# A four-layer graph network on one core: table look-ups as float32r parts, and a row-by-row dilation in blocks of 32 rows on GpSimd

## The chip, the core and the metric

The kernel runs on one core of a Trainium2 chip. A core has five engines with an instruction queue each: TensorE (PE, matrix products; PEld is its weight load), VectorE (DVE), ScalarE (ACT), GpSimd (POOL) and SyncE (SP, which here only issues DMA transfers). Each engine works its queue off in order and waits on semaphores for the others. The metric is the time of one execution on the device in microseconds (us), the median of several runs.

## The reference, cut to what matters

There are 16 graphs of 1024 nodes with 128 features and a 0/1 adjacency `adj` of 1024x1024 per graph. Four layers follow one another, each of the form `x = layernorm(x + layer(x, adj))`:

- layer 0: attention with relu projections, masked by `adj`;
- layer 1: a maximum over neighbours. With `q = x W2`, each node takes `max_j adj[i,j] * relu(p_i + q_j + b)`;
- layer 2: a sum over neighbours and two dense layers;
- layer 3: three rounds of neighbour averaging, normalisation and batch norm, on a *dilated* adjacency.

The dilation depends on `adj` alone, and it is sequential. For each row n, in order:

```
row  = carry[n]                 # earlier rows' removals are already in it
num  = sum(row)
sf   = (num + 1) // 2 if num > 10 else 1
rm   = row & (cumsum(row) % sf == 0)     # none if num <= 1 or masked
carry[n]    = row & ~rm
carry[:, n] = carry[:, n] & ~rm          # also in the later rows
```

So row n removes its neighbours of rank sf and 2 sf (or all of them), and what it removes in column n changes the counts and ranks of the later rows.

## The kernel before

**Layers 0 to 2** (function `layers_012`) run graph by graph. The loop over the graphs calls `max_conv(b)` for layer 1. Its inner loop has 147 groups `g` of 7 nodes each. For every 21 groups DVE builds `sub`, the maxima of all 128 subsets of 7 values of `q` (line 270). Three groups at a time are transposed by PE (line 277) and copied by ACT to an SBUF tile `table` (line 279, three buffers). For each group, PE counts with a bf16 product which subset of the 7 nodes each of the 1024 nodes has as neighbours (`pm`, line 284, a PSUM tile with one buffer), ACT turns that into the 0/1 tile `hot` (line 286), PE looks the maxima up by a product of `table` and `hot` in float32 (`pg`, line 150, called from `look_up`), and DVE takes the running maximum `best` (line 262).

After every group, `between(g)` puts in pieces of other work: layer 2 of the graph before (`gin`), layer 0 of the graph after (`attention`), and the dilation, a generator that yields after each piece. `pieces` and `slots` spread its pieces evenly over the 16 x 147 groups in the order of the source. The framework then schedules each engine's queue itself, by data dependences and its own estimates, so the order on an engine can differ from that of the source.

**The dilation** works in 8 blocks of 128 rows of all graphs. A block loads its rows as bytes (`E`, partition = row in the block, graph and column in the free dimension) and the squares on the diagonal (`Dg`, partition = graph). It takes off what earlier blocks removed (`rp`, transposed by PE, line 353, subtracted by DVE, line 354), counts the rows outside the square by ACT (lines 356 and 360), and then does 127 steps, one per row, on 16 partitions, all on DVE (lines 374 to 387): a running count over the 128 columns of the square (a scan), five instructions on one element per graph, three over the row, and one over the column below, in bytes. The square goes back to `E` through DRAM (`own`, lines 391 and 392), ACT counts again (line 396), and a scan over the whole row with an ACT instruction and one DVE instruction (lines 413 to 416) marks what each row removes. That is stored to `removed` (line 418).

GpSimd has little to do: `off` for attention (line 219), the small vectors of `layernorm` and its 8 wide instructions (lines 161 to 171), and the loads that convert a type.

**Layer 3** reads `removed` per graph in one transfer (`gone_all`, line 492), takes it and its transpose off the adjacency (`dilated`, lines 499 and 500), and runs `sage` per graph and round, with two reciprocals on DVE in the first round (`deg`, line 513, and `inv`, line 532). `deg` is stored as `share` (line 514).

Of the kernel before, what the change touches and what calls it, by code (L numbers as in the profile page):

```python
# [26 lines left out]
F32 = mybir.dt.float32  # L28
BF = mybir.dt.bfloat16
# [7 lines left out]
P = 128  # L37
# [5 lines left out]
TG = 21  # L43
LOWEST = -(2.0**100)
# [17 lines left out]
def tile_graph_layers(ctx: ExitStack, tc, a, out):  # L62
# [11 lines left out]

    def bank(name, dtype=F32):
        return psum.tile([P, 2048 // (2 if dtype == BF else 4)], dtype, tag="bank", name=name, bufs=2)

# [44 lines left out]
    mask_u = consts.tile([B, N], U8, name="mask_u")  # L122
    nc.sync.dma_start(out=mask_u, in_=a["nodemask"])
    half_mask = consts.tile([B, N], F32, name="half_mask")
    nc.vector.tensor_scalar(half_mask, mask_u, 0.5, None, op0=ALU.mult)
    nm = consts.tile([P, T, B], F32, name="nm")
    half_nm = consts.tile([P, T, B], F32, name="half_nm")
# [3 lines left out]
    nc.vector.tensor_copy(half_nm.rearrange("p t b -> p (t b)"), pm[:, :T * B])  # L131
    nc.vector.tensor_scalar_mul(nm, half_nm, 2.0)
# [3 lines left out]
    removed = [dram.tile([N, N], BF, name=f"removed{b}") for b in range(B)]  # L136
# [16 lines left out]
    def layernorm(dst, src):  # L153
# [9 lines left out]
        gp.tensor_scalar(mean, mean, 0.5, None, op0=ALU.mult)  # L163
# [3 lines left out]
        gp.tensor_scalar(apart, apart, 0.25, None, op0=ALU.mult)  # L167
        gp.tensor_add(var, var, apart)  # L168
        gp.tensor_tensor(rs, var, mhalf, op=ALU.pow)  # L169
        for t in range(T):  # L170
            gp.tensor_scalar(dst[:, t, :], src[:, t, :], mean[:, t:t + 1], rs[:, t:t + 1],  # L171
                             op0=ALU.subtract, op1=ALU.mult)
# [20 lines left out]
    def layers_012():  # L193
# [6 lines left out]
        def attention(b, An):  # L200
# [6 lines left out]
            nc.gpsimd.tensor_scalar_mul(kT, kT, -1.0)  # L207
# [40 lines left out]
        def max_conv(b, AT, between):  # L248
# [8 lines left out]
            def look_up(g, table, hot):  # L257
                pg = product(table, hot, "pg")
                if g == 0:
                    nc.vector.tensor_copy(best, pg)  # L260
                else:
                    nc.vector.tensor_max(best, best, pg)  # L262

            last = None
            for g0 in range(0, NG, TG):
# [6 lines left out]
                for g in range(g0, g0 + TG):  # L272
                    at = (g - g0) % 3
                    if at == 0:
                        pt = bank("pt")
                        for k in range(3):
                            nc.tensor.transpose(pt[:, k * P:(k + 1) * P], sub[:, g - g0 + k, :], ident)  # L277
                        table = w2.tile([P, 3, P], F32, name="table", bufs=3)
                        nc.scalar.copy(table.rearrange("s g o -> s (g o)"), pt[:, :3 * P])  # L279
# [5 lines left out]
                    hot = w2.tile([P, N], F32, name="hot", bufs=2)  # L285
# [3 lines left out]
                    last = g, table[:, at, :], hot  # L289
# [45 lines left out]

        def dilation():
            for k in range(T):
                own = slice(k * P, (k + 1) * P)
                E = dil.tile([P, B, N], U8, name="E")
                nc.gpsimd.dma_start(out=E, in_=adj[:, own, :].rearrange("b p m -> p b m"))  # L340
                Dg = dil.tile([B, P, P], U8, name="Dg")
                nc.gpsimd.dma_start(out=Dg, in_=adj[:, own, own])

                counts = dil.tile([P, 2, B], F32, name="counts")
                nc.vector.memset(counts, 0.0)
                for b in range(B):
                    if k:
                        rp = dil.tile([P, T - 1, P], BF, name="rp", bufs=2)
                        nc.sync.dma_start(out=rp[:, :k, :],
                                          in_=removed[b][:k * P, own].rearrange("(j p) n -> p j n", p=P))  # L350
                        p = bank("pr", BF)
                        for j in range(k):
                            nc.tensor.transpose(p[:, j * P:(j + 1) * P], rp[:, j, :], ident_b)
                        nc.vector.tensor_tensor(E[:, b, :k * P], E[:, b, :k * P], p[:, :k * P], op=ALU.is_gt)
                        junk = dil.tile([P, N], BF, name="junk", tag="gone", bufs=2)
                        nc.scalar.activation(junk[:, :k * P], E[:, b, :k * P], AF.Copy,
                                             accum_out=counts[:, 0, b:b + 1])
                    if k < T - 1:
                        junk = dil.tile([P, N], BF, name="junk", tag="gone", bufs=2)
                        nc.scalar.activation(junk[:, :N - (k + 1) * P], E[:, b, (k + 1) * P:], AF.Copy,  # L360
                                             accum_out=counts[:, 1, b:b + 1])
                    yield
                p = bank("pc")
                for s in range(2):
                    nc.tensor.transpose(p[:B, s * P:(s + 1) * P], counts[:, s, :], ident)
                before = dil.tile([B, P], F32, name="before")
                after = dil.tile([B, P], F32, name="after")
                nc.vector.tensor_scalar_add(before, p[:B, 0:P], 1.0)
                nc.vector.tensor_scalar_add(after, p[:B, P:2 * P], -0.5)
                for n in range(P - 1):  # L370
                    mine = Dg[:, n, :]
                    m = slice(k * P + n, k * P + n + 1)
                    rank1 = small.tile([B, P], F32, name="rank1")
                    nc.vector.tensor_tensor_scan(rank1, mine, mine, before[:, n:n + 1], op0=ALU.add, op1=ALU.max)  # L374
                    sc = small.tile([B, 5], F32, name="sc")
                    half, h1, at, every, at2 = (sc[:, i:i + 1] for i in range(5))
                    nc.vector.tensor_scalar(half, rank1[:, P - 1:P], after[:, n:n + 1], half_mask[:, m],
                                            op0=ALU.add, op1=ALU.mult)
                    nc.vector.tensor_scalar(h1, half, MAGIC, 1.0 - MAGIC, op0=ALU.add, op1=ALU.add)
                    nc.vector.scalar_tensor_tensor(at, half, 5.5, h1, op0=ALU.is_gt, op1=ALU.mult)  # L380
                    nc.vector.scalar_tensor_tensor(every, half, 1.0, at, op0=ALU.is_gt, op1=ALU.is_gt)
                    nc.vector.tensor_scalar(at2, at, 2.0, -1.0, op0=ALU.mult, op1=ALU.add)
                    hit = small.tile([B, P], F32, name="hit")
                    nc.vector.tensor_scalar(hit, rank1, at, every, op0=ALU.is_equal, op1=ALU.max)  # L384
                    nc.vector.scalar_tensor_tensor(hit, rank1, at2, hit, op0=ALU.is_equal, op1=ALU.max)  # L385
                    nc.vector.tensor_mul(hit, hit, mine)
                    nc.vector.tensor_tensor(Dg[:, n + 1:, n], Dg[:, n + 1:, n], hit[:, n + 1:], op=ALU.is_gt)  # L387
                    yield

                Dd = dram.tile([B, P, P], U8, name=f"own{k}")  # L390
                nc.sync.dma_start(out=Dd, in_=Dg)
# [231 lines left out]
```

## Time and profile before

| what | value |
|---|---|
| median of 3 runs | 9725.1 us (9717.61 to 9733.46) |
| the profiled execution's own time | 9721.92 us |
| its span, first to last instruction | 9720.1 us |
| mean granted TensorE clock | 0.932 of full speed |
| PE busy | 8365.7 us, 86% of the span |
| DVE busy | 7624.2 us, 78% |
| ACT busy | 4286.9 us, 44% |
| POOL busy | 1095.8 us, 11%, 1423 instructions |
| stores of `x3` (end of a graph's layer 2), first and last | 679.1 and 7887.9 us |

Busy shares are of the whole span. The first 7888 us belong to layers 0 to 2 with the dilation beside them, the rest to layer 3. Times in the views are microseconds, means are nanoseconds. A group's line gives line, engine, operation, the tiles written and read, shapes, count, busy time and mean, and then the idle time of the engine just before these instructions and what ended most of it. A line of a timeline gives start and length.

### The profile page before, as it was taken

How to read it: one execution, taken by the hardware profiler on the slowest of the kernel's cores; microseconds unless marked ns; L12 is line 12 of the kernel's file. 1: busy time of each engine (PE TensorE's matmuls, PEld its weight loads, DVE VectorE, ACT ScalarE, POOL GpSimd, SP SyncE). 2: the span in 40 equal slices, each digit the busy share in tenths (PEclk: the TensorE clock that was granted, in tenths of full speed). 3: DMA queues.
4: the chain of work that ended last, by engine and by line, in shares of the span. 5: the costliest groups of instructions: out<-in, count | busy, mean ns of one | idle time of the engine just before them, and what ended most of it. 6: DMA issues, size and time to landing. Idle time of an engine off the chain costs nothing. (4 is left out here: it accounts for less than half of the span.)

```text
span 9720.1 us, 86636 instructions
## 1 busy us (share of the span) xinstructions
PE 8365.7 (86%) x29288; PEld 4084.1 (42%) x29288; DVE 7624.2 (78%) x16197; ACT 4286.9 (44%) x5170; POOL 1095.8 (11%) x1423
## 2 busy tenths in 40 slices
PE   7989898999899989898989898989898967778774
PEld 4444444444444444444444444444444433334333
DVE  4998599869886988699859986998699958845454
ACT  3445544554465445444554455445544621122221
POOL 1010101010101010101010101010101010101116
PEclk8999999999999999999999999999999978889886
DMA  3010201020102010201020102010200057733332
GB/s 47 1 22 19 35 1 22 19 37 1 22 20 39 1 22 20 40 1 22 19 43 1 22 18 46 1 22 18 47 1 11 11 159 201 200 115 130 130 130 75
DMA packets 317237, 435.20 MB, mean 45 GB/s; under 512 B 105445, under 2 KB 156792, under 8 KB 316662
## 3 DMA queue, kind: packets, MB, share of 16 engines
q1 hardware_dynamic: 219696, 295.75, 9.2%
q0 software_dynamic: 92560, 132.72, 8.8%
q8 instruction: 230, 3.77, 0.2%
q10 hardware_dynamic: 4534, 1.19, 0.1%
q14 instruction: 217, 1.78, 0.1%
HBM read 461.64 MB, written 119.54 MB: 60 GB/s over the span
## 5 line engine op out<-in xcount | busy, mean ns | idle before, releaser
L150 PE MATMUL pg<-hot,table 128*128 128x512 f32 x9408 | 4548.7, 605 | 134.4 <-DVE best L262 42.8
L286 ACT ACTIVATE hot<-pm,one_less 128x1024 f32<-128x1024 f32 x2352 | 2617.1, 1113 | 2235.1 <-PE pm L284 2080.4
L262 DVE TENSOR_TENSOR best<-best,pg 128x1024 f32<-128x1024 f32 x2336 | 2828.8, 1211 | 534.5 <-PE pg L150 530.4
L150 PEld LDWEIGHTS pg<-hot,table 128*128 128x128 f32 x9408 | 1729.4, 191 | 1770.3 <-issue 1137.5
L284 PE MATMUL pm<-AT,lit 126*128 126x512 bf16 x4704 | 1437.2, 385 | 190.9 <-ACT hot L286 101.3
L284 PEld LDWEIGHTS <-lit 126*128 126x128 bf16 x4704 | 461.0, 99 | 1099.8 <-issue 1067.1
L279 ACT COPY table<-pt 128x384 f32<-128x384 f32 x784 | 373.3, 477 | 816.5 <-PE pt L277 811.5
L219 POOL TENSOR_SCALAR off<-An 128x1024 bf16<-128x1024 bf16 x128 | 164.2, 1283 | 3578.7 <-PE psc L223 3183.0
L277 PE MATMUL pt<-ident,sub 128*128 128x128 f32 x2352 | 410.8, 283 | 178.3 <-DVE sub L270 88.6
L189 PE MATMUL pagg<-m,part 128*128 128x512 bf16 x2304 | 529.0, 382 | 34.9 <-DVE inv L530 25.4
L277 PEld LDWEIGHTS pt<-ident,sub 128*128 128x128 f32 x2352 | 304.4, 146 | 516.6 <-issue 270.2
L374 DVE TENSOR_TENSOR_SCAN rank<-Dg,before 16x128 f32<-16x128 uint8 x1016 | 498.4, 491 | 27.2
L270 DVE TENSOR_TENSOR sub<-sub,q 128x21 f32<-128x21 f32 (+6 forms) x784 | 434.9, 555 | 49.3 <-ACT q L252 43.9
L387 DVE TENSOR_TENSOR Dg<-Dg,hit 16x127 uint8<-16x127 uint8 (+63 forms) x1016 | 454.2, 447 | 24.5
L189 PEld LDWEIGHTS <-part 128*128 128x128 bf16 x3072 | 298.2, 98 | 394.9 <-issue 53.4
L385 DVE SCALAR_TENSOR_TENSOR hit<-rank,sc,hit 16x128 f32<-16x128 f32 x1016 | 348.1, 343 | 25.6
L557 PE MATMUL pl<-w_L_gnn_Wl,hT 128*128 128x128 f32 x768 | 199.1, 367 | 178.6 <-ACT hT L581 113.2
L178 ACT CAST part<-left 128x1024 bf16<-128x1024 f32 x128 | 133.7, 1044 | 482.9 <-DVE left L180 482.8
L384 DVE TENSOR_SCALAR hit<-rank,sc 16x128 f32<-16x128 f32 x1016 | 342.7, 337 | 0.0
L532 DVE RECIPROCAL inv<-inv 128x1024 f32<-128x1024 f32 x48 | 314.3, 6548 | 19.3 <-ACT inv L531 19.3
L560 DVE SCALAR_TENSOR_TENSOR x<-pl,nm,x 128x128 f32<-128x128 f32 x384 | 129.5, 337 | 252.2 <-PE pl L557 161.4
L171 POOL TENSOR_SCALAR X<-y,ln_mv 128x128 f32<-128x128 f32 x384 | 319.4, 848 | 5.2
(172 smaller groups left out, 8512.2 us busy)
## 6 DMA issues: line engine op xcount, KB each, us to landing
m<-kept SPq DMA_DIRECT2D x32, 2048.0 KB, 9.4
An<-in_adj_dram POOLq DMA_DIRECT2D x16, 2048.0 KB, 14.3
removed<-gone SPq DMA_DIRECT2D x128, 256.0 KB, 2.0
m<-in_adjT_dram POOLq DMA_DIRECT2D x16, 2048.0 KB, 13.6
gone_all<-removed SPq DMA_DIRECT2D x16, 2048.0 KB, 9.7
kept<-m SPq DMA_DIRECT2D x16, 2048.0 KB, 14.2
AT<-in_adjT_dram POOLq DMA_DIRECT2D x16, 2016.0 KB, 14.6
hidden<-r SPq DMA_DIRECT2D x48, 512.0 KB, 3.8
```

The costliest lines, as they stand in the source:

```text
L150: nc.tensor.matmul(p[:, s], lhsT, rhs[:, s], start=True, stop=True)
L189: nc.tensor.matmul(p[:, s], parts[k][:, c, :], m[:, c, s], start=(c == 0 and k == 0), stop=(c == T - 1 and k == 2))
L262: nc.vector.tensor_max(best, best, pg)
L270: nc.vector.tensor_max(sub[:, :, n:2 * n], sub[:, :, 0:n], qg[:, g0:g0 + TG, k:k + 1].to_broadcast([P, TG, n]))
L277: nc.tensor.transpose(pt[:, k * P:(k + 1) * P], sub[:, g - g0 + k, :], ident)
L279: nc.scalar.copy(table.rearrange("s g o -> s (g o)"), pt[:, :3 * P])
L284: nc.tensor.matmul(pm[:, s], lit[:rows, r, :], AT[:rows, c, s], start=True, stop=True)
L286: nc.scalar.activation(hot, pm, AF.Relu, bias=one_less)
L374: nc.vector.tensor_tensor_scan(rank1, mine, mine, before[:, n:n + 1], op0=ALU.add, op1=ALU.max)
L384: nc.vector.tensor_scalar(hit, rank1, at, every, op0=ALU.is_equal, op1=ALU.max)
L385: nc.vector.scalar_tensor_tensor(hit, rank1, at2, hit, op0=ALU.is_equal, op1=ALU.max)
L387: nc.vector.tensor_tensor(Dg[:, n + 1:, n], Dg[:, n + 1:, n], hit[:, n + 1:], op=ALU.is_gt)
```

## The change

**Look-up.** The transposed table goes to two tiles of type float32r, a shortened float32 for PE. ACT copies it to `high` (which rounds) and, whole, to `whole`; GpSimd writes the difference to `low`. `hot` becomes float32r too. `look_up` makes four float32r products per group (two halves, `high` and `low` each) in place of two in float32.

**Dilation.** Blocks have 32 rows instead of 128, so there are 32 blocks. Four graphs are packed on 128 partitions: partition = 32 g + row, with graph = 4 q + g. Loads come one block ahead, and the next block is prepared by the generator `prepare` among the steps of the current one. DVE ranks the ones above the diagonal of the 32x32 squares once per block and writes to `V` (through DRAM, partition = graph) for each such pair its rank from the row's start in the square, or a large number where there is no pair. A step then no longer needs the row itself, only the count `low` of what lies before the diagonal and the count `rest` of the whole row: ten GpSimd instructions, six on one element per graph and four on the rest of the row. The hits of a block go back through DRAM, DVE transposes them in 32x32 squares, and the whole-row part at the end of a block is as before, but with four rows of 1024 per block and partition and with DVE transposing the removals (`last_T`, stored to `removed_T`) in place of PE. `pieces` follows the new count.

**Elsewhere.** `layernorm` and the negation of `kT` use multiply and add on GpSimd. Sixteen small transfers fill `half_rows` at the start. `gone_all` comes in four transfers of 32 partitions each, since `removed` is laid out by block.

The core of the diff:

```diff
-            def look_up(g, table, hot):
-                pg = product(table, hot, "pg")
+            def look_up(g, parts, hot):
+                pg = wide("pg")
+                for s in halves:
+                    for k, part in enumerate(parts):
+                        nc.tensor.matmul(pg[:, s], part, hot[:, s], start=(k == 0), stop=(k == 1))
...
-                        table = w2.tile([P, 3, P], F32, name="table", bufs=3)
-                        nc.scalar.copy(table.rearrange("s g o -> s (g o)"), pt[:, :3 * P])
+                        high = w2.tile([P, 3 * P], F32R, name="high", bufs=2)
+                        nc.scalar.copy(high, pt[:, :3 * P])
+                        whole = w2.tile([P, 3 * P], F32, name="whole")
+                        nc.scalar.copy(whole, pt[:, :3 * P])
+                        low = w2.tile([P, 3 * P], F32R, name="low", bufs=2)
+                        nc.gpsimd.tensor_sub(low, whole, high.bitcast(F32))
...
-                    hot = w2.tile([P, N], F32, name="hot", bufs=2)
+                    hot = w2.tile([P, N], F32R, name="hot", bufs=2)
...
-                for n in range(P - 1):
-                    mine = Dg[:, n, :]
...
-                    nc.vector.tensor_tensor_scan(rank1, mine, mine, before[:, n:n + 1], op0=ALU.add, op1=ALU.max)
...
-                    nc.vector.tensor_mul(hit, hit, mine)
-                    nc.vector.tensor_tensor(Dg[:, n + 1:, n], Dg[:, n + 1:, n], hit[:, n + 1:], op=ALU.is_gt)
+                gp = nc.gpsimd
+                for n in range(R - 1):
+                    if n % 4 == 3 and k + 1 < K:
+                        next(ahead, None)
+                    m = slice(k * R + n, k * R + n + 1)
+                    mine = low[:, n:n + 1]
+                    sc = small.tile([B, 6], F32, name="sc")
+                    half, sf, none, at, to = (sc[:, i:i + 1] for i in range(5))
+                    gp.tensor_scalar(half, mine, half_mask[:, m], rest[:, n:n + 1], op0=ALU.mult, op1=ALU.add)
+                    gp.tensor_scalar(sf, half, MAGIC, -MAGIC, op0=ALU.add, op1=ALU.add)
+                    gp.tensor_scalar(sf, half, 5.5, sf, op0=ALU.is_gt, op1=ALU.mult)
+                    gp.tensor_scalar(none, half, 1.0, FAR, op0=ALU.is_le, op1=ALU.mult)
+                    gp.tensor_sub(at, mine, sf)
+                    gp.tensor_scalar(to, at, sf, none, op0=ALU.subtract, op1=ALU.subtract)
+                    last = small.tile([B, R], F32, name="last_rank")
+                    gp.tensor_scalar(hit[:, n, n + 1:], V[:, n, n + 1:], at, None, op0=ALU.is_equal)
+                    gp.tensor_scalar(last[:, n + 1:], V[:, n, n + 1:], to, None, op0=ALU.is_le)
+                    gp.tensor_add(hit[:, n, n + 1:], hit[:, n, n + 1:], last[:, n + 1:])
+                    gp.tensor_sub(low[:, n + 1:], low[:, n + 1:], hit[:, n, n + 1:])
                     yield
...
-            gp.tensor_scalar(dst[:, t, :], src[:, t, :], mean[:, t:t + 1], rs[:, t:t + 1],
-                             op0=ALU.subtract, op1=ALU.mult)
+            gp.tensor_scalar(dst[:, t, :], src[:, t, :], rs[:, t:t + 1], mean[:, t:t + 1],
+                             op0=ALU.mult, op1=ALU.add)
...
-        pieces, slots, done = T * (3 * B + P - 1), B * NG, 0
+        pieces, slots, done = K * (R + 8), B * NG, 0
...
-        nc.sync.dma_start(out=gone, in_=removed[b].rearrange("(c p) i -> p c i", p=P))
+        q, g = divmod(b, G)
+        rows = removed[:, g * R:(g + 1) * R, q, :].rearrange("(c k) r i -> k r c i", c=T)
+        for k in range(P // R):
+            nc.sync.dma_start(out=gone[k * R:(k + 1) * R], in_=rows[k])
```

## The prediction, made before the changed kernel ran

> **What bounds the kernel now.** I read the page's busy shares, then stretches of time, the costliest groups, one stretch of the timeline, and last GpSimd's (POOL's) own timeline. Layers 0 to 2 run from 0 to 7888 us (the last store of `x3` is issued there, line 331); layer 3 takes the other 1832 us. One graph of layers 0 to 2 has 147 look-up groups, which I call slots. From the first `x3` store (679.1) to the fifteenth (7505.6) there are 14 graphs: 487.6 us each. The busy time by stretches of 240 us, columns length, PE, PEld, DVE, ACT, POOL, clock, DMA:
>
> ```profile
> 1200.00:1440.00 240.00, 221.64 (x764) 107.20 (x762) 230.01 (x599) 111.56 (x130) 10.69 (x8) 0.99 0.00 1
> 1440.00:1680.00 240.00, 212.85 (x675) 97.43 (x675) 218.19 (x614) 102.98 (x112) 35.35 (x55) 0.95 0.11 23
> 1680.00:1920.00 240.00, 222.74 (x751) 109.51 (x750) 210.69 (x448) 138.00 (x170) 15.02 (x9) 0.97 0.08 14
> 1920.00:2160.00 240.00, 211.50 (x728) 102.98 (x729) 146.04 (x198) 127.96 (x186) 34.74 (x56) 0.94 0.25 43
> ```
>
> Of two graphs, three stretches have DVE at 210 to 230 of 240 us and PE at 213 to 223: two engines near their limit. The fourth, without dilation steps, has PE alone at 212. POOL is nearly empty. The groups that matter (times, busy and mean, idle before):
>
> ```profile
> L150 PE MATMUL pg<-hot,table 128*128 128x512 f32 x9408 | 4548.7, 605 | 134.4 <-DVE best L262 42.8
> L286 ACT ACTIVATE hot<-pm,one_less 128x1024 f32<-128x1024 f32 x2352 | 2617.1, 1113 | 2235.1 <-PE pm L284 2080.4
> L262 DVE TENSOR_TENSOR best<-best,pg 128x1024 f32<-128x1024 f32 x2336 | 2828.8, 1211 | 534.5 <-PE pg L150 530.4
> ...
> L279 ACT COPY table<-pt 128x384 f32<-128x384 f32 x784 | 373.3, 477 | 816.5 <-PE pt L277 811.5
> ...
> L374 DVE TENSOR_TENSOR_SCAN rank<-Dg,before 16x128 f32<-16x128 uint8 x1016 | 498.4, 491 | 27.2
> ```
>
> One slot in a stretch without dilation:
>
> ```profile
> 2004.16 0.60 PE L284 MATMUL pm<-AT,lit 126*128 126x512 bf16 x2
> ...
> 2004.59 1.88 PE L150 MATMUL pg<-hot,table 128*128 128x512 f32 x4
> 2004.85 1.11 ACT L286 ACTIVATE hot<-pm,one_less 128x1024 f32<-128x1024 f32 x1 [1.04 <-PE pm L284]
> ...
> 2006.31 0.60 PE L284 MATMUL pm<-AT,lit 126*128 126x512 bf16 x2
> ```
>
> Start to start, two bf16 products take 0.43 us (0.215 each) and the two f32 products, four records, 1.72 us (0.43 a record). The period is 2.15; with the transposes (0.32 start to start per three slots, 0.11 a slot) 2.26. PE sets it and ACT waits. `hot` starts 0.69 after `pm` and runs 1.11, and `pm` has one buffer.
>
> POOL's small instructions, in a quiet stretch (start, length):
>
> ```profile
> 117.18 0.24 POOL L163 TENSOR_SCALAR ln_mv<-ln_mv 128x8 f32<-128x8 f32 x1
> 117.38 0.20 POOL L164 TENSOR_TENSOR ln_mv<-ln_mv 128x8 f32<-128x8 f32 x1
> 117.66 0.20 POOL L166 TENSOR_SCALAR ln_mv<-ln_mv 128x8 f32<-128x8 f32 x1
> 117.95 0.24 POOL L167 TENSOR_SCALAR ln_mv<-ln_mv 128x8 f32<-128x8 f32 x1
> 118.27 0.20 POOL L168 TENSOR_TENSOR ln_mv<-ln_mv 128x8 f32<-128x8 f32 x1
> 118.55 1.68 POOL L169 TENSOR_TENSOR ln_mv<-ln_mv,mhalf 128x8 f32<-128x8 f32 x1
> ```
>
> From 164 on, where each needs a result just made, starts lie 0.28, 0.29, 0.32 and 0.28 apart. The step of the new dilation is such a chain.
>
> **Part 1: DVE is relieved.** The ten step instructions (lines 374 to 387) were busy 2778 us, 174 per graph. DVE was busy 6299.6 of the 7480 us from 120 to 7600, 411 per graph; 237 stay. The new block work adds little: per block some 25 instructions of at most 128 elements, nearest the 16x1 to 16x128 rows (134 to 343 ns), about 6 us, and four transposes of up to 992 bf16 elements, by the 672-element row (0.86 us) at most 1.3 us each; the other forms shrink or stay. Even at 260 us DVE no longer sets the end.
>
> **Part 2: the look-up.** Four f32 records of 0.43 become four float32r matmuls. The trace has no such operand. Its bounds are the bf16 product (0.215) and the f32 record (0.43). I take 0.215: an f32 product costs four bf16 ones, as when both operands are cut in two, and here the kernel does the cutting itself, with one matmul per part. A slot then asks PE for 0.43 + 0.86 + 0.11 = 1.40 us. What is late next is the loop of the one `pm` buffer: 0.69 + 1.11 + about 0.06 for the release = 1.86 us. ACT has 0.69 free in it, into which one table copy (0.48) fits; there are now two per three slots, so I add 0.48 / 3 = 0.16: 2.02 us a slot.
>
> By the Trainium skill, page FP8 and Floating Point Precision, section TensorE Precision Notes, true FP32 takes four passes and FP32 can be read at reduced precision instead. The four passes agree with 0.86 against 0.215 us here; the page names no float32r, and no run yet shows the reduced read. One pass is the sum as I make it, two are the second rival below.
>
> **Part 3: a step on POOL.** Ten instructions, nine of which need the result before them. At the spacing above: 9 x 0.29 + 0.17 (the distance of independent ones) = 2.8 us. Four of them are on 31 down to 1 elements, 16 on average: the row of `inv` (line 535, 128x1024, 2828 ns) against 0.20 for 8 elements gives 2.6 ns an element, so 4 x 16 x 2.6 = 0.17. That is 2.95 us. Seven operands are per-partition scalars read from SBUF. Line 171 has two of them on 128 elements and a median of 803 ns: 128 x 2.6 = 333 and 0.22 leave 0.25, so 0 to 0.13 each. Step: 2.95 to 3.85 us; I take 3.3, since line 171 also has a second operation that may take that rest.
>
> The Trainium skill, GPSIMD Engine Reference, section 4.1 Engine selection, speaks against the move: elementwise work belongs on VectorE, with GpSimd about twice as slow for two inputs. Here DVE's 16x1 instructions took 134 to 158 ns and POOL's 200 to 240, 1.5 times. Twice 145 ns would be 2.9 us a step as an estimate, about 400 us less in the whole than my 3.3.
>
> **Part 4: where the steps stand.** This decides. Every third slot `low<-whole,high` is now queued on POOL, and PE can't look up without it. Its cost: 0.20 + 376 x 2.6 ns = 1.17 us. In POOL's order of the built program a graph in the middle has 49 of these and two blocks of 31 steps, but the steps are not spread: the 31 stand in runs of 19, 7, 1, 4 in one block and 1, 13, 6, 5, 6 in the other, with one `low` between runs. Only 7 of the 49 lie inside blocks, 42 (126 slots) outside. `low` and `high` have two buffers, `whole` one. So while POOL works off 19 steps (63 us), PE has two tables at most, 12 us of work, and then waits. The cover that hid `low` is gone there; the queue behind a step is every `low`, `off` and load on POOL, and behind those PE, ACT and DVE. Block time and slot time add:
>
> - blocks: 62 x 3.3 = 204.6, and 7 x 1.17 = 8.2: 213 us;
> - 126 slots x 2.02 = 254.5;
> - other ACT work, in the same loop: ACT was busy 3694 of 7480 us, 241 a graph, of which `hot` and table were 187; 54 are left, less the old counts (lines 356, 360 and 396: some 354 us, 22 a graph), plus the new ones (128 of about 0.8 us, 6.5): 38.5;
> - seams between graphs: PE was busy 6765.8 of 7480 us, so it waited 46.5 us a graph, which I keep.
>
> Sum 552.8 against 487.6: 65.2 x 16 = **+1043 us**.
>
> **Part 5: the ends.** Layer 3's first pass took 37.7 us a graph (`deg` on DVE, line 513, at 8133.38 and 8171.05). Each graph's `gone_all` comes in four loads now, and in SP's order the fourth stands behind the `share` store of the graph before, thus behind the reciprocal `deg` (line 513, 6.54 us). That exposes up to the landing (9.7 us, line 492) plus the 6.5: 0 to 16 us a graph. I take 12: +192. The layernorm's 8 wide instructions change to multiply-add, whose row (`off`, 1283 ns for 1024) gives about 0.4 instead of 0.80 us; where POOL sets the end (9561 to 9715 us) that is up to 16 x 8 x 0.4 = 51, I take -42. Sixteen more loads on POOL ahead of the first `An` cost about 1 us each by line 427's row (1017 ns): +15. The wait of hits for their two hops through DRAM (own's hops: 3.8 and 3.9 us) lies under the 21 tables between blocks, some 130 us: nothing; without that cover it is 32 x 8 = 256.
>
> Sum: 9720.1 + 1043 + 192 - 42 + 15 = 10,928 us. The profiled run's own time was 9721.92 and the median 9725.1, so +5: **10,930 us**.
>
> **Rivals.**
> 1. *Faster: a POOL step is cheap.* Only 16 of 128 partitions and mostly one element; independent instructions start 0.17 apart. The point: 62 s + 348 = 487.6 - 10 (part 5) gives s = 2.1 us. At 1.6 us, ten at 0.16: 10,930 - 62 x 1.7 x 16 = 9,240. Against: one element still took 228 ns (line 546), and dependent starts in that stretch never lay under 0.28. Chance 0.08.
> 2. *float32r at 0.43.* PE sets the slot again: 0.43 + 1.72 + 0.11 = 2.26, so 126 x 0.24 = 30 a graph, +484: 11,415. For: every f32 record, the transposes too (0.107 per 128 columns), runs at half the bf16 rate. Chance 0.15.
> 3. *Scalar operands at 0.13 each.* s = 3.85: +546, 11,475. For: line 171. Chance 0.17.
>
> **How the numbers follow.** The forecast has 0.60, from 2.4 to 3.5 us a step. The low end is 2.4 us, where the wait on the result before cost almost nothing: -893, 10,040, rounded to 10,000. The high end, 11,750, holds each of rivals 2 and 3 and a part of both together (11,960). Outside are rival 1 and the rest of that. What a measurement of this kernel can tell from no change is about 0.2%, 20 us. Faster 0.07, same 0.01 (rival 1 near its point), slower 0.92.
>
> **What would show it.** POOL busy near half the span with some 10,000 instructions of 0.2 to 0.35 us; PE's wait for `low` on POOL at the head of the waits, in pieces of 10 to 50 us, 100 us or more a graph; DVE near half busy; a graph's period near 550 us with two stretches of about 100 us in which PE is nearly idle and its clock may fall; the look-up's records 0.215 apart, and `hot` still waiting for `pm`. I am wrong if POOL's step is under 2.1 us, or if PE's waits for POOL are short.

## The result and the profile after

| | before | changed |
|---|---|---|
| median of the comparison's runs | 9721.35 us (9717.45 to 9733.46) | 11144.93 us (11134.22 to 11147.04) |
| ratio to before, 95% interval | | 1.146 (1.144 to 1.148) |
| span of the profiled execution | 9720.1 us | 11132.5 us |
| mean granted TensorE clock | 0.932 | 0.808 |
| layers 0 to 2, last store of `x3` | 7887.9 us | 9080.2 us |
| a graph, first to fifteenth store, 14 graphs | 487.6 us | (8703.15 - 802.7) / 14 = 564.3 us |
| layer 3, from that last store to the end | 1832 us | 2052 us |

The change is slower by 14.6%. The prediction was 10,930 us, 2% below what was measured. The page after, busy shares and four rows of slices:

```profile
PE 7135.3 (64%) x28909; PEld 4339.3 (39%) x29144; DVE 5552.6 (50%) x7044; ACT 4337.4 (39%) x5498; POOL 4462.2 (40%) x12357
...
PE   5666666666666666666666666666666655558776
...
DVE  3545454545454545454544545454545455555555
...
POOL 5444544444444444444444444444444510001114
```

DVE fell from 78% to 50%, as the edit says it should, and yet the kernel is longer. No engine is near full in any slice of layers 0 to 2. That is the look of a kernel that waits. The groups that answer to those of before (busy and mean, then idle before and its releaser):

```profile
L290 DVE TENSOR_TENSOR best<-best,pg 128x1024 f32<-128x1024 f32 x2336 | 2843.8, 1217 | 3221.7 <-PE pg L286 3195.7
...
L286 PE MATMUL pg<-hot,low 128*128 128x512 f32 x4704 | 2031.4, 435 | 2100.1 <-POOL low L311 2100.1
...
L311 POOL TENSOR_TENSOR low<-whole,high 128x384 fp32r<-128x384 f32 x784 | 799.4, 1020 | 2510.9 <-ACT whole L309 2401.9
```

`low` itself takes 1.02 us, 50 us a graph. But PE stood 2100.1 us idle before the products with `low`, and the view of waits gives the longest piece:

```profile
PE pg L286 <- POOL low L311: 2100.1, 230, 49.2
...
ACT whole L309 <- POOL low L311: 1403.1, 146, 44.5
```

Columns are the sum, the number and the longest. These are 131 us a graph, and few waits make it: of 15 in the graph that ends at 7001 us, five last 11 to 49 us and 119 us together. What POOL does meanwhile is a step, and the next, with no `low` between them. One step in POOL's timeline (start, length), from line 469 to the next line 469:

```profile
3001.82 0.32 POOL L469 TENSOR_SCALAR sc<-low_counts,half_mask,rest 16x1 f32<-16x1 f32 x1
...
3003.43 0.37 POOL L474 TENSOR_SCALAR sc<-sc 16x1 f32<-16x1 f32 x1
...
3004.77 0.19 POOL L479 TENSOR_TENSOR low_counts<-low_counts,hit 16x9 f32<-16x9 f32 x1
3005.07 0.33 POOL L469 TENSOR_SCALAR sc<-low_counts,half_mask,rest 16x1 f32<-16x1 f32 x1
```

It lasts 3.25 us here, 3.5 us on the longest rows, 3.33 on average where nothing comes between; I use 3.35. And PE in the same block, at the end of such a wait:

```profile
2983.59 0.58 PE L286 MATMUL pg<-hot,high 128*128 128x512 f32 x1
2995.33 0.80 PE L286 MATMUL pg<-hot,low 128*128 128x512 f32 x1 [11.17 <-POOL low L311]
2995.93 0.63 PE L286 MATMUL pg<-hot,high 128*128 128x512 f32 x1
2996.35 0.63 PE L286 MATMUL pg<-hot,low 128*128 128x512 f32 x1
...
3001.65 0.40 PE L286 MATMUL pg<-hot,low 128*128 128x512 f32 x1
3001.88 0.39 PE L286 MATMUL pg<-hot,high 128*128 128x512 f32 x1
```

PE gets one `low`, works off three slots in 8 us, and waits for the next `low` behind the next run of steps (11.5 us at 3015.12). The second thing to see is the spacing: 0.42 us right after the wait, 0.23 us six microseconds later. I come back to that in the last section.

### The profile page after: what moved, and what is told of

Same layout as the page of the kernel before. It is cut to its first block, busy times and chain, and to the rows that moved or that the text cites. A ratio compares the mean times of both kernels' runs of the same rounds, so it can differ in the third digit from the quotient of the medians.

```text
span 11132.5 us, 90950 instructions
## 1 busy us (share of the span) xinstructions
PE 7135.3 (64%) x28909; PEld 4339.3 (39%) x29144; DVE 5552.6 (50%) x7044; ACT 4337.4 (39%) x5498; POOL 4462.2 (40%) x12357
## 5 line engine op out<-in xcount | busy, mean ns | idle before, releaser
L318 ACT ACTIVATE hot<-pm,one_less 128x1024 fp32r<-128x1024 f32 x2352 | 2621.2, 1114 | 2793.6 <-PE pm L316 1726.8
L286 PE MATMUL pg<-hot,low 128*128 128x512 f32 x4704 | 2031.4, 435 | 2100.1 <-POOL low L311 2100.1
L286 PE MATMUL pg<-hot,high 128*128 128x512 f32 x4704 | 2402.0, 514 | 133.7 <-DVE e L252 67.6
L286 PEld LDWEIGHTS pg<-hot,low 128*128 128x128 f32 x4704 | 990.5, 211 | 2363.4 <-POOL low L311 2184.4
L311 POOL TENSOR_TENSOR low<-whole,high 128x384 fp32r<-128x384 f32 x784 | 799.4, 1020 | 2510.9 <-ACT whole L309 2401.9
L286 PEld LDWEIGHTS pg<-hot,high 128*128 128x128 f32 x4704 | 971.8, 208 | 610.1 <-DVE best L290 100.8
L309 ACT COPY whole<-pt 128x384 f32<-128x384 f32 x784 | 382.8, 488 | 1404.5 <-POOL low L311 1403.1
L307 ACT CAST high<-pt 128x384 fp32r<-128x384 f32 x784 | 373.0, 476 | 329.5 <-PE pt L305 297.4
L474 POOL TENSOR_SCALAR sc<-sc 16x1 f32<-16x1 f32 x992 | 374.7, 378 | 109.6
L476 POOL TENSOR_SCALAR hit<-V,sc 16x31 bf16<-16x31 bf16 (+30 forms) x992 | 347.7, 351 | 0.0
L471 POOL TENSOR_SCALAR sc<-sc 16x1 f32<-16x1 f32 x992 | 289.1, 291 | 108.2
```

Of the source, the lines that this page charges most:

```text
L286: nc.tensor.matmul(pg[:, s], part, hot[:, s], start=(k == 0), stop=(k == 1))
L307: nc.scalar.copy(high, pt[:, :3 * P])
L309: nc.scalar.copy(whole, pt[:, :3 * P])
L311: nc.gpsimd.tensor_sub(low, whole, high.bitcast(F32))
L318: nc.scalar.activation(hot, pm, AF.Relu, bias=one_less)
L474: gp.tensor_scalar(to, at, sf, none, op0=ALU.subtract, op1=ALU.subtract)
```

## The experiments

My theory after the result had a narrow and a wide form. Narrow: only `low`, queued behind steps, costs the time. Wide: GpSimd works its queue in order, so whatever is computed on GpSimd or issued from it stands behind a run of steps, and every engine stands behind that. The rivals were that the block-wise dilation is slow wherever its steps run, that GpSimd's work slows VectorE, and that layer 3 is slow for a reason of its own. Periods below are always from the first to the fifteenth `x3` store, over 14 graphs; some of the expectations have 492, 425 and 540 us for kernels that have 490.0, 432.0 and 552.3 by this measure. A time without a range is that of one execution; kernels that ran four to seven times spread by 0.1 to 0.3%.

**The look-up alone.** The kernel before with the float32r tables (`rank1` and `hit` have one buffer, for space).

```diff
-                        table = w2.tile([P, 3, P], F32, name="table", bufs=3)
...
+                        high = w2.tile([P, 3 * P], F32R, name="high", bufs=2)
...
+                        nc.gpsimd.tensor_sub(low, whole, high.bitcast(F32))
```

> The old dilation (blocks of 128 rows, steps on DVE) with the new look-up: high and whole copied by ACT, low on GpSimd, four float32r products a group. To make room, rank1 and hit of the old steps have one buffer each. Theory (GpSimd's queue is the cause): GpSimd carries no steps, so low comes on time; PE's group costs 1.40 us in place of 2.26, but DVE stays near its limit (411 of 487.6 us a graph), so the period falls only a little, to 455 to 485 us, and the time is 9250 to 9700 us; PE's waits for low are under 100 us in all. Rival (the look-up itself costs, through two copies and a third engine): period above 500, time above 9900 us.

Measured 9862.6 us (before in this comparison: 9726.45), 1.4% slower. The period was 497.2 us, the last store came at 7866.1 as before, and what remained of the dilation delayed layer 3: its first `deg` stood at 8073.0 instead of 7931.1. I had expected a gain, and that was a miss. DVE stayed at 79% with the old steps, so a shorter slot on PE had little to give: with these steps on DVE the look-up was not what set the end. And the steps themselves grew, from 2778 to 3034 us of instruction time, nearly all of it in instructions that ran while GpSimd computed a `low`; the last section shows one. So the look-up's part on GpSimd did slow VectorE here. How much of the 1.4% comes from that, no run tells.

**The dilation alone.** The changed kernel with the float32 table, so that nothing of the look-up is on GpSimd.

> The new dilation with the old look-up in float32 (table by one ACT copy, nothing of it on GpSimd). Theory in its narrow form (only low behind the steps holds PE up): a group costs PE 2.26 us, 147 of them 332 us, with 109 us of PE for attention and layer 2 and 46 us of waits a period of 487 us, and with 220 us for layer 3's change a time of about 9950 us. Theory in its wide form (everything behind the steps on GpSimd holds up the graph: layernorm and off of attention stand behind whole blocks too): a period above 540 us, a time above 10800 us, with PE's or ACT's waits on GpSimd's off and layernorm. Rival (float32r is what slows the kernel): time at or below 9720 us.

Measured 11877.87 us, period 608.9. Slower than the changed kernel, although no `low` exists. The narrow form falls here. The head of its waits names who waits now, which isn't `off` or the layernorm, as I had written:

```profile
DVE hit_T L484 <- DMA hit_p<-hit: 2367.8, 32, 77.7
```

There are 32 blocks, and 32 waits of 74 us on average. `hit_T` transposes the hits of a block, and in DVE's order it stands long before the steps are done; every `best` behind it waits too.

**`low` on VectorE.** The changed kernel, with `low` computed on DVE from PSUM.

```diff
-                        whole = w2.tile([P, 3 * P], F32, name="whole")
-                        nc.scalar.copy(whole, pt[:, :3 * P])
-                        nc.gpsimd.tensor_sub(low, whole, high.bitcast(F32))
+                        nc.vector.tensor_sub(low, pt[:, :3 * P], high.bitcast(F32))
```

> The changed kernel with low computed by DVE from PSUM (pt minus high), without the copy whole; steps stay on GpSimd. Narrow form: PE no longer waits for GpSimd, a group takes the 1.86 us of the pm loop, 147 x 1.86 + 85 = 358 us a graph, a time of about 7900 us. Wide form: layernorm and off wait behind blocks of 31 steps (104 us each) and the period stays above 490 us, a time above 9900 us. Rival (the look-up's work, not the queue): no change from 11145 us beyond 3%.

Measured 10947.96 us, period 552.3 instead of 564.3. PE no longer waits 2100 us for `low`, and the time came back almost whole as the same wait as above, in this kernel 2319.1 us of DVE for `hit_p`, 75.4 us at most. By its number alone, 1.8% from the changed kernel, this run also fits the rival that I had named (the look-up's own work, within 3%); the runs with the steps on VectorE and without steps below, which keep that work and are fast, rule it out.

**The hits not awaited.** As the last one, and `hit_p` is loaded from another tensor, so that `hit_T` need not wait, and `low_counts` and `rest` have two buffers (the removals are then others).

```diff
-                                      in_=hit_d.rearrange("(q g) n m -> g n q m", g=G)[g])
+                                      in_=above_d[k].rearrange("(q g) n m -> g n q m", g=G)[g])
...
-                low = dil.tile([B, R], F32, name="low_counts")
+                low = dil.tile([B, R], F32, name="low_counts", bufs=2)
```

> Steps on GpSimd, `low` on VectorE as in the run with `low` on VectorE (10948 us, where `hit_T` on VectorE waited 2319 us for the hits, 75 us at most), and now nothing waits for the hits: `hit_p` is loaded from the block's `above` matrix instead of the hits (the hits are computed and stored, and not used), and `low_counts` and `rest` have two buffers, so that the next block's counts need not wait for the steps either. Theory A (`low` and `hit_T` are the waits that cost): with both gone the period falls from 540 us a graph to the 405 to 425 us that the kernel has without the steps or with the steps on VectorE, 9000 to 9150 us in all. Theory B (the steps hold whatever else stands in GpSimd's queue, and no two waits hold all of it): the loads of `E` for the next block, `off` and the layernorm are issued or computed on GpSimd behind the same steps, so the wait moves to them; the gain is below 400 us, 10550 to 10900 us in all, and VectorE and ScalarE are then seen to wait for `E` or for `off`'s followers in pieces of 30 us and more.

Measured 10828.02 us, 120 us less, all of it after the fifteenth `x3` store; the period is 551.2. Theory B. In the waits of this kernel the place of `hit_T` is taken by the bytes of the next block:

```profile
DVE square L399 <- DMA E<-in_adj_dram: 1786.8, 31, 87.6
ACT junk L428 <- DMA E<-in_adj_dram: 1365.9, 20, 88.3
```

Nothing in the data makes `E` wait for a step. It is the queue: GpSimd issues these loads, and in its timeline the four issues follow the block's last step at once, while DVE has idled for 85.9 us:

```profile
2162.47 0.18 POOL L477 TENSOR_TENSOR low_counts<-low_counts,hit 16x1 f32<-16x1 f32 x1
2162.96 2.34 POOL L382 DMA_DIRECT2D E<-in_adj_dram  x4 [0.32 <-issue]
...
2172.64 0.23 DVE L399 CAST square<-E 128x128 bf16<-128x128 uint8 x1 [85.90 <-DMA E<-in_adj_dram]
```

So the changed kernel, the one without `low` on GpSimd's queue and the one in which `hit_T` doesn't wait either have periods of 564.3, 552.3 and 551.2 us. The wait moves, and its longest pieces, 75 and 88 us, are most of a block's 31 x 3.35 = 104 us.

**The steps on VectorE.** The changed kernel with one name changed; `low` stays on GpSimd.

```diff
-                gp = nc.gpsimd
+                gp = nc.vector
                 for n in range(R - 1):
```

> The changed kernel with the ten instructions of a step on DVE in place of GpSimd, all else the same (low stays on GpSimd). Theory (the steps' place on GpSimd is the cause): GpSimd is free for low, off and layernorm; DVE has some 260 us a graph and 62 steps of about 1.8 us (by the old 16x1 rows, 134 to 158 ns, and 0.03 for each wait) = 112 more, 372 us; with waits a period of 375 to 440 us and a time of 8100 to 9200 us, under the kernel before. Rival (32 blocks with their hops through DRAM, or the look-up, cost the time): above 9700 us.

Measured 9046.98 us (9037.1 to 9051.4), ratio to before 0.930 (0.928 to 0.931), period 432.0. The same blocks, counts, hops through DRAM and look-up are 7% faster than before instead of 14.6% slower, so the dilation in blocks isn't slow by itself. DVE's timeline, one step:

```profile
1529.80 0.26 DVE L469 TENSOR_SCALAR sc<-low_counts,half_mask,rest 16x1 f32<-16x1 f32 x1
...
1530.23 1.20 DVE L290 TENSOR_TENSOR best<-best,pg 128x1024 f32<-128x1024 f32 x1
...
1531.96 1.20 DVE L290 TENSOR_TENSOR best<-best,pg 128x1024 f32<-128x1024 f32 x1
...
1533.76 1.20 DVE L290 TENSOR_TENSOR best<-best,pg 128x1024 f32<-128x1024 f32 x1
...
1535.27 0.26 DVE L469 TENSOR_SCALAR sc<-low_counts,half_mask,rest 16x1 f32<-16x1 f32 x1
```

A step takes 5.5 us from start to start, longer than on POOL. But three look-ups pass within it, because on this engine the order puts `best` between a step's instructions. PE's wait for `low` is 154.5 us instead of 2100.1. In busy time a step adds (7100.4 - 5552.6) / 992 = 1.56 us to DVE, where it added (4462.2 - 1784.7) / 992 = 2.70 us to POOL. The lengths of its instructions add up to 2.12 and 2.78 us; on DVE they partly lie over one another and over `best`.

**A longer and a shorter step.** Three dependent instructions more, and, in the other kernel, four instructions in place of ten: seven go, and one of another form computes `at` (the removals are then others).

```diff
                     gp.tensor_scalar(half, mine, half_mask[:, m], rest[:, n:n + 1], op0=ALU.mult, op1=ALU.add)
+                    for _ in range(3):
+                        gp.tensor_scalar(half, half, 1.0, 0.0, op0=ALU.mult, op1=ALU.add)
```

> The changed kernel with three more GpSimd instructions in each step, each needing the one before (half times 1 plus 0, on 16x1). By the row of line 190 (204 ns) and the 0.08 us of a wait they are 0.28 to 0.30 us each, 0.87 a step. Theory (block time and group time add, 62 steps a graph in series with the rest): 62 x 0.87 = 54 us a graph, +860 us, 12010 us, a step of 4.2 us. Rival (the steps lie beside other work, and fixed hops of a block set the time): under +250 us, below 11400 us.

> The changed kernel with six of the ten instructions of a step left out (the rounding of sf, the limit, none, the second rank and the sum of hits), so the removals are not those of the reference; queues, loads, block count and hops through DRAM are the same. Four instructions of the measured lengths and their waits are 1.55 us a step in place of 3.35. Theory (steps add in series): 62 x 1.8 = 112 us a graph, -1790 us, about 9360 us, below the kernel before, as the prediction's point of 2.1 us says. Rival (fixed hops): above 10700 us.

Measured 11601.79 us with steps of 4.1 us on average, period 593.0; and 9941.92 us with steps of 1.64 us, period 490.0. Both lie between theory and rival. The time goes with the step both ways, and less than the full 62 steps a graph: 28.7 us of some 48 added, 74.3 us of 105 removed. In GpSimd's queue of the longer step the scheduler had put more `low` between the steps, in that of the shorter step fewer. So an edit of the step also edits the order, and a slope from such pairs isn't that of one fixed queue.

**No steps.** The ten instructions left out, all else in place (the hits stay zero).

> The changed kernel without the ten GpSimd instructions of a step: the hits stay zero, all other work of the block, its hops through DRAM and the float32r look-up with `low` on GpSimd remain. It measures what is left when a step costs nothing. Additive theory of the prediction: block time and slot time add, so a graph loses 62 x 3.35 = 208 us, 564.3 - 208 = 356 us a graph, and the whole is near 11145 - 16 x 208 = 7820 us. By the slope seen with four of ten instructions, (564.3 - 492) / 1.7 = 42.5 us of a graph per us of a step: 564.3 - 3.35 x 42.5 = 422 us a graph, 8870 us in all, near the period of 425 us that the kernel had with the steps on VectorE; the steps then cost 142 us a graph where they have 208 us of instructions. Rival (something other than the steps limits it from 1.65 us down): a period above 470 us and more than 9600 us in all.

Measured 8727.59 us, period 412.5. PE's wait for `low` is then

```profile
PE pg L286 <- POOL low L311: 148.4, 169, 3.4
```

The steps cost 564.3 - 412.5 = 151.8 us a graph, where they have 62 x 3.35 = 208 us of instructions: 73% shows. The additive theory's 7820 us was far off, the slope's 8870 near. DVE was busy 5599.5 us here and 5552.6 us with the steps on GpSimd, so the rival that GpSimd's steps slow VectorE down finds nothing in these two totals.

**Layer 3, the store elsewhere.** The store of `share` goes out from GpSimd's queue, so that the fourth piece of `gone_all` is no longer behind it; in the changed kernel and in the one with the steps on VectorE.

```diff
-            nc.sync.dma_start(out=share[b], in_=deg)
+            nc.gpsimd.dma_start(out=share[b], in_=deg)
```

> The changed kernel with the store of share issued on GpSimd's queue in place of SP's, so that no load of gone_all stands behind it. Theory (the fourth piece of gone_all waits behind the reciprocal): the first pass of layer 3 falls from 54.5 us a graph (deg on DVE, first to last 818 us over 15) to 38 to 42, -200 to -270 us, 10875 to 10945 us. Rival (the loads of 32 partitions are slower in themselves, or the masks of DVE): the pass stays above 50 us a graph, above 11070 us.

> Steps on DVE (9047 us) together with the store of share on GpSimd's queue. If the two are independent: 9047 - 235 = 8810 us, 8770 to 8870, a ratio of 0.902 to 0.912 to the kernel before. If the share store is not what holds layer 3's first pass: 9030 to 9060 us.

Measured 11133.75 us (against 11144.93) and 9043.03 us (9030.73 to 9045.04, against 9046.98): no gain in either. The queue behind `share` is not the cause.

**Layer 3, one load.** `removed` is stored per graph, in four stores of 32 rows each, and `gone_all` comes in one load; with the steps on VectorE and in the changed kernel.

```diff
-        for k in range(P // R):
-            nc.sync.dma_start(out=gone[k * R:(k + 1) * R], in_=rows[k])
+        nc.sync.dma_start(out=gone, in_=removed[b].rearrange("(c p) i -> p c i", p=P))
```

> The steps are on VectorE and the removals are stored per graph again, in four stores of 32 rows for each q, so that layer 3 fetches a graph's `gone_all` in one load. Theory (the four loads make the longer pass): with four loads the first pass of layer 3 took 54.5 us a graph, with one load, in the kernel before, 37.7 to 38.3. The pass returns to 38 us a graph, 15 to 16 x 16.5 = 250 to 265 us less than the 9047 of the steps on VectorE: 8785 us, between 8740 and 8840; layers 0 to 2 still end near 6990, since the four stores for one lie on SP, which waits more than it works. Rival (the pass is long for another reason, the masks' new order on VectorE and TensorE among the layernorm's changed instructions): 9045 us, pass still above 50 us a graph.

> The changed kernel with `gone_all` in one load and the removals stored per graph; the steps stay on GpSimd. Theory (the four loads): layer 3's first pass goes from 54.5 to 38 us a graph, 250 to 265 us less than 11145: 10885 us, between 10840 and 10940, with layers 0 to 2 ending near 9080 as in the changed kernel. Rival (not the loads): 11140 us. A third outcome would be that only one of the two kernels of this call gains, which would make it a matter of order and not of the loads.

Measured 8782.27 us (8773.23 to 8796.16), ratio to before 0.9025 (0.901 to 0.904), and 10895.3 us: 265 and 250 us less. Both within what the theory said. The first and last `deg` of the sixteen, in the changed kernel and then in the same kernel with one load:

```profile
L628 DVE RECIPROCAL deg<-deg x16: 6552/6553/6554, 9143.5 to 9961.3; 128x1024 f32<-128x1024 f32 x16
```

```profile
L626 DVE RECIPROCAL deg<-deg x16: 6536/6537/6553, 9139.2 to 9710.4; 128x1024 f32<-128x1024 f32 x16
```

817.8 / 15 = 54.5 us a graph, and 571.2 / 15 = 38.1 us; before it was 38.3. The kernel with the steps on VectorE and one load beats both kernels of the comparison, by 9.75% the one before.

## Why the prediction was right, and where it was not

**Right: the sign, the mechanism, most of the size.** The step measured 3.35 us for my 3.3. A scalar operand from SBUF costs little: the instruction with one such operand (line 471) had a mean of 291 ns against 233 for the one without (line 470), the two with two (lines 469 and 474) 329 and 378. So the seven operands are some 0.05 to 0.07 us each, the middle of my 0 to 0.13, and the third rival fell. The float32r records lay 0.23 us apart (3141.92, 3142.15, 3142.38), near my 0.215 and far from 0.43; the second rival fell. The first rival's cheap step, 1.6 us, never came: the shortest that I found took 3.16 us. PE's wait for `low` came in pieces up to 49 us and 131 us a graph, DVE fell to half.

**The total by its parts.** Layers 0 to 2 became 1192 us longer, where I had 1043 + 15; layer 3 220 us, where I had 192 - 42. The misses are 134 and 70 us, 204 of the 215 us between prediction and result.

**Failed: "block time and slot time add".** The sum was 62 x 3.3 = 204.6 us for steps and 348 for the rest. The kernel without steps puts the rest at 412.5, and the steps at 151.8, as far as two kernels with different orders on GpSimd's queue can be subtracted. The rest was 64 us too small and the steps were charged 53 us too much. These two errors cancelled; that the total of 552.8 (its terms add up to 552.5) came near 564.3 was luck. The cover I denied exists: 27% of the steps' time lies beside other work, and from the first to the last step of a block PE was busy for 36 to 55 of 110 us, where I had called it nearly idle. That the rest is larger isn't due to the slot: undisturbed slots follow each other in 1.86 us (`pm` at 3143.04, 3144.90, 3146.76), less than my 2.02, since both table copies fit into ACT's free time. All 147 slots at 1.86 us are 273 us, so 139 us are left for what I had put at 85 (46.5 us of seams and 38.5 us of other ACT work, both taken over from the kernel before). The trace of the kernel without steps shows where they lie, from `pm` to `pm`, on the mean of twelve graphs: 92 us in the 39 slots of a graph in which PE also works for attention or layer 2 (busy with that for 87 us), 33 us in the other slots, 14 us between graphs. So the term that my sum put at nothing is PE's own work for the other layers: it makes the slots that hold it longer, instead of fitting into the time that `pm`'s loop leaves PE.

**Failed: the break-even of 2.1 us.** With steps of 1.64 us the kernel still took 9942 us. A point between that kernel and the one without steps gives an estimate of 1.3 us: the period would have to be 474 us, which is 487.6 less layer 3's 220 / 16, and (474 - 412.5) / ((490.0 - 412.5) / 1.64) = 1.3.

**Failed: "the wait of hits lies under the 21 tables between blocks: nothing".** In the changed kernel DVE waited 289.0 us for the hits, in 32 waits of 9 us on average, near the 32 x 8 = 256 that I had named for the case without cover; how much of that the kernel's time shows, no run tells. Take `low` off GpSimd's queue, and the same hits hold DVE for 2319 us. And my naming of one follower was too narrow: `low` was the wait that ended last, not the cause.

**Layer 3: size nearly, place wrong.** I took 12 us a graph from bounds of 0 to 16, for a piece of `gone_all` behind `share`. The order was as I said: `share` is issued at 9585.32 and the piece at 9585.71. But moving `share` gained nothing, and one load instead of four gained 38.1 against 54.5, 16.4 us a graph, just past the upper bound. The four loads are the cause, or the layout that needs them. In the trace with one load, DVE takes the masks of a graph in pieces between the reciprocals and round work of others; with four, most of them stand in one block after them. Whether that order comes first or the landing (12.0 us for a quarter by the page of the profile, 9.8 us for the single load) wasn't separated. The layernorm's -42 held: from the last `deg` to the end it took 1214.6 us before, 1171.2 after; in the other kernels with this layernorm it took 1170 to 1189, so 26 to 44 us.

**The two rules.** By the Trainium skill, page GPSIMD Engine Reference, section 4.1 Engine selection, elementwise work with two inputs is about twice as slow on GpSimd, and with one input roughly at line rate. Seven of a step's ten instructions have one tensor input, and on 16x1 they are slower on GpSimd too: line 470 takes 233 ns there and 138 on VectorE, 1.7 times, as the busy time that a step adds (2.70 and 1.56 us); the lengths added up (2.78 and 2.12 us) give 1.3. But the factor explains little: GpSimd had the time free. What it hadn't was a free queue. By the page FP8 and Floating Point Precision, section TensorE Precision Notes, FP32 can be read at reduced precision instead of four passes; the runs have float32r at 0.23 us a record, near the 0.215 of bf16 and as such a read would give, against 0.43 for each of the two records of a float32 product.

**Together, not apart.** The look-up alone lost 1.4%, the dilation alone gave 11877.87, 22% more than before, both together 14.6%. The two halves change each other's worth: with the old steps on DVE the shorter slot gained nothing, and with the new steps on GpSimd it gives 733 us. I read this from the sum: slots that must fit between the blocks then count in full; no run shows it by itself. With the steps on DVE the two halves together gain 7%; the new dilation there without the new look-up wasn't run.

## What to carry to other kernels

An idle engine isn't a free one: its queue is in order, so before a long dependent chain is moved to it, list everything else computed on it or issued from it, and ask how soon each is wanted. If taking one follower away only renames the wait at the head of the view of waits, the cause is the queue; move the chain, not the follower. Here the chain was cheaper on the busier engine: there the order let the critical work pass between its instructions, while on GpSimd the others stood behind runs of up to 19 steps.

## What the runs showed of the hardware

**The clock after a wait.** After the long waits of PE for `low`, PE ran at half its rate for some microseconds. In the timeline above, after 11.17 us of idle time, float32r records lie 0.42 us apart from 2995.93 to 2999.95, and 0.23 from 3001.65 on. Windows of the changed kernel show the granted clock beside it (columns: length, busy PE, PEld, DVE, ACT, POOL, then clock, DMA share, GB/s):

```profile
2945.00:2975.00 30.00, 0.80 (x3) 0.27 (x2) 0.41 (x1) 0.30 (x1) 24.50 (x87) 0.58 0.00 0
3120.00:3150.00 30.00, 25.65 (x117) 16.49 (x117) 19.25 (x25) 19.21 (x25) 5.69 (x6) 1.00 0.00 1
4139.00:4178.00 39.00, 29.79 (x85) 19.26 (x86) 15.66 (x34) 8.35 (x10) 17.08 (x60) 0.50 0.01 2
```

In this trace the clock is only ever 1.0 or 0.5. In layers 0 to 2 all 84 waits for `low` of over 4 us ended at 0.5, and none of the 8 of 2 to 2.5 us did. The Trainium skill, page TensorE: Matmul & The Clock Gate, section What's actually happening, says that TensorE falls to half its clock after an idle window and comes back after about 3.4 us of sustained work. The trace agrees for the fall, and after 72 of the 84 waits full rate came back within 2.9 to 8.2 us. After the other 12, one in each of twelve graphs, it took 39 to 43 us, although PE was busy for most of it: the third row has 29.8 of 39 us. What sets these apart, no run tells.

Slots follow in 2.57 us (`pm` at 2977.44 and 2980.01) instead of 1.86 at half the clock. Over the 14 graphs the mean clock was 0.81, and 0.96 before, which is 215 and 40 us of half clock a graph. PE was busy in 84 and 25 of these; at full rate that work would still have taken at least half as long, so the change lost up to (84 - 25) / 2, some 30 us a graph, by the clock, an estimate from these numbers. My sum had no such term. It is a cost of waits that the waits themselves don't show.

**GpSimd and VectorE at once.** In the kernel with the look-up alone, the same step instruction on DVE, without and with a `low` on GpSimd beside it:

```profile
3702.52 0.28 DVE L394 TENSOR_TENSOR hit<-hit,Dg 16x128 f32<-16x128 f32 x1
...
3706.12 1.04 POOL L287 TENSOR_TENSOR low<-whole,high 128x384 fp32r<-128x384 f32 x1 [0.59 <-ACT whole L285]
3706.31 0.99 DVE L394 TENSOR_TENSOR hit<-hit,Dg 16x128 f32<-16x128 f32 x1
```

The 103 of the 1016 such instructions that met a `low` took 705 ns on average, the others 282; in the kernel before none took over 281. Seven of the ten instructions of the old step show it, and the three TENSOR_SCALAR ones on 16x1 don't (255 ns with a `low` beside them and 257 without, for one). With the new steps on VectorE it is there too: line 473 takes 668 ns beside a `low` and 147 else, and the instructions that show it add some 200 us to DVE's time. `low` and the steps both on VectorE wasn't run.
